# Talking-heads attention with soft mixture of experts, fp32, one core: TensorE's order within a pair of query blocks, pinned, twelve slots for rows, and the norm of mu made per batch

## Chip, cores and metric

The kernel runs on one core of a Trainium2 chip. The metric is the device time of one execution in microseconds. Before the change it is 9190.56 us, the median of three runs (9187.51, 9190.56 and 9199.91).

## The reference

The input x is 4 x 2048 x 256 in fp32, with 16 heads of 16 in the attention and 16 experts of 16 slots each in the mixture. In short, for each of the four batches:

```python
q, k, v = split(x @ Wqkv.T + bqkv)          # 16 heads of 16; rope on q and k
l = einsum('bhij,gh->bgij', q @ k.T * SCALE, Wpre)   # heads mixed before the softmax
a = einsum('bhij,gh->bgij', softmax(l), Wpost)       # and after it
x = layernorm(x + (a @ v) @ Wout.T + bout)
xn = layernorm(x) * gamma + beta
logits = (xn / |xn| * scale) @ (mu / |mu|)  # |mu| over the 256 rows of each of 256 columns
# dispatch = softmax over tokens' experts, combine = softmax over all slots;
# gelu experts on the dispatched slots, combined back
x = layernorm(x + combine(experts(dispatch(xn))))
```

## The kernel before

A batch is done in three stages, one batch after another: `qkv` (projections and rope, about 80 us), `attention` (2058 to 2068 us from the first q k to the last product with v) and `moe` (the mixture and both norms around it, about 160 us). Everything is fp32. Each fp32 matmul appears as two weight loads and two passes in the trace.

The attention walks over 128 **pairs** n of a batch. A pair is two blocks x of 8 query rows, and a block holds 16 heads x 8 queries = 128 rows. The 2048 keys are split into two halves j. TensorE has four kinds of work per pair:

- **q k** (tile `s`, L366, `raw_banks`): the raw scores of a pair. 16 matmuls on 32x32 tiles of the array per half, over all four row groups r and four column groups q, in the order r, then q. Row group r writes PSUM bank r of the four that it takes. The four banks are copied to `raw` in SBUF (L529 on DVE, L532 on ACT).
- `raw_rows` (L388) then moves `raw` into `rows` by eight DMAs of 256 KB on SP's queue, which brings the heads of a query onto the partitions. The DMAs of x=0 and x=1 and of halves j=0 and j=1 go into four separate slots of the ring `rows`.
- **Wpre** (tile `l`, L406, `logits`): 16 matmuls on 32x32 tiles per half mix the heads of those rows; they go through row groups 0 to 3 in turn and write two tiles (x = 0, 1) of two banks each. DVE takes each tile's maximum (`top`, L421) and ACT the exponential with that maximum as bias (`expo`, L430), written over the same slot of `rows`.
- `shares` and `weights` put the maxima and sums of both halves together (DVE L441 and L455, ACT L444, POOL L443 to L458) into `w`, which holds Wpost with the softmax's factors in it.
- **mixing** (tile `t`, L478, `mix`): 16 matmuls of 128x128 per half mix the heads behind the softmax and transpose; the four banks go to `aT` by DVE and ACT.
- **v's product** (tile `o`, L498, `values`): 64 matmuls, 128x32 tiles, for half of the heads of one group of 32 query rows in each pair; two copies (L509, L510) put it into `aoT`. After every eighth pair, `finish` (L522 on) multiplies 128 rows by Wout (`pz`), adds the residual `xr` and takes the norm's statistics.

PSUM has four banks with tag `t`, shared in turn by q k, mixing, v's product and `pz`, and two tiles of two banks for Wpre. A matmul that gets a bank waits until what was in it has been copied out.

The order within an iteration n is written out: for each half j, Wpre of pair n, q k of pair n+2, then mixing of pair n-1, block x = j, both of its halves; after the second half `raw_rows(n + 2)` and v's product; at the end the shares. The engines' copies, maxima and exponentials are pinned to that order by `keep_in_program_order` (`keep`); the matmuls, the reciprocal, the two copies of v's product and the shares are not, though the trace shows the phases in the order given. The ring `rows` has ten slots of which a pair takes four; `raw`, `w` and `aT` have two. A second ring `k1` of six slots serves qb (the queries, made by POOL at L343 two pairs ahead), `aoT`, and short-lived tiles of the other two stages. The normalised mu (`mun`) is made once at the start (L134 to L145) and stays in SBUF.

In `moe`, DVE takes the statistics of the norm over 16 tiles (L229, L235), ACT the root (L237), and the normalised rows go through POOL (L604, L605) and ACT (L607) before TensorE has its next work. The stores of the output (L711) and the loads of the next batch's x (L251) share SP's queue.

Of the kernel before, what the change touches and what calls it, by code (L numbers as in the profile page):

```python
# [25 lines left out]
def kernel(  # L26
# [35 lines left out]
    ROWS = 10  # L62
# [38 lines left out]
    mu_sb = work.tile([P, KC, ES], F32, tag="rows", name="mu_sb", bufs=ROWS)  # L101
    nc.scalar.dma_start(mu_sb, mu.rearrange("(c p) e -> p c e", p=P))
# [5 lines left out]
    ones = work.tile([P, P], F32, tag="k1", name="ones", bufs=6)  # L108
    nc.gpsimd.memset(ones, 1.0)
# [23 lines left out]

    sq = work.tile([P, KC, ES], F32, tag="rows", name="sq", bufs=ROWS)  # L134
    nc.vector.tensor_mul(sq, mu_sb, mu_sb)
    pn = ps_t.tile([P, 512], F32, tag="t", name="pn")
    for c in range(KC):
        nc.tensor.matmul(pn[:, :ES], ones, sq[:, c], start=(c == 0), stop=(c == KC - 1))
    rmu = work.tile([P, ES], F32, tag="k1", name="rmu", bufs=6)
    nc.scalar.activation(rmu, pn[:, :ES], AF.Sqrt)  # L140
    nc.vector.tensor_scalar_max(rmu, rmu, NORM_EPS)
    nc.vector.reciprocal(rmu, rmu)
    mun = const.tile([P, KC, ES], F32, tag="mun", name="mun")
    for c in range(KC):
        nc.vector.tensor_mul(mun[:, c], mu_sb[:, c], rmu)  # L145


# [13 lines left out]

    def k1(shape, name):
        return work.tile(shape, F32, tag="k1", name=name, bufs=6)
# [85 lines left out]
    def load_x(b, t, name):  # L249
        xt = work.tile([P, D], F32, tag="x", name=f"{name}_{b}_{t}", bufs=2)  # L250
        nc.sync.dma_start(xt, x[b, ts(t, P), :])  # L251
        return xt


    def qkv(b):
        room = work.tile([P, NT * HEADS * GI], F32, tag="aT", name=f"wq_{b}")
        wqkv_sb, bqkv_sb, rope_sb = carve(room, [KC, 3 * D], [3 * D], [NT, 4 * HH])
        nc.scalar.dma_start(wqkv_sb, wqkvT.rearrange("(c p) n -> p c n", p=P))
        nc.scalar.dma_start(bqkv_sb, bqkv.partition_broadcast(P))
        nc.scalar.dma_start(rope_sb, rope.rearrange("(t p) k -> p t k", p=P))  # L260
        qT = seq.tile([P, NT, KC, P], F32, tag="qT", name=f"qT_{b}")
        kT = seq.tile([P, KC, N], F32, tag="kT", name=f"kT_{b}")
        v = seq.tile([P, NT, D], F32, tag="v", name=f"v_{b}")

        def project(t):
            xt = load_x(b, t, "x")
            px = ps_t.tile([P, 4, P], F32, tag="t", name=f"px_{b}_{t}")
            for c in range(KC):
                nc.tensor.transpose(px[:, c, :], xt[:, ts(c, P)], ident)
            xT = k1([P, KC, P], f"xT_{b}_{t}")  # L270
            nc.scalar.copy(xT, px[:, :KC, :])
            pqk = ps_t.tile([P, 512], F32, tag="t", name=f"pqk_{b}_{t}")
            pv = ps_t.tile([P, 512], F32, tag="t", name=f"pv_{b}_{t}")
            for c in range(KC):
                nc.tensor.matmul(
                    pqk[:, : 2 * D], xT[:, c, :], wqkv_sb[:, c, : 2 * D],
                    start=(c == 0), stop=(c == KC - 1),
                )
            for c in range(KC):
                nc.tensor.matmul(  # L280
                    pv[:, :D], xT[:, c, :], wqkv_sb[:, c, 2 * D :],
                    start=(c == 0), stop=(c == KC - 1),
                )
            qk = k2([P, 2 * HEADS, 2, HH], f"qk_{b}_{t}")
            nc.vector.tensor_add(  # L285
                qk.rearrange("p h a d -> p (h a d)"), pqk[:, : 2 * D], bqkv_sb[:, : 2 * D]
            )
            nc.vector.tensor_add(v[:, t, :], pv[:, :D], bqkv_sb[:, 2 * D :])

            cc = rope_sb[:, t, : 2 * HH].unsqueeze(1).to_broadcast([P, 2 * HEADS, 2 * HH])  # L290
            ss = [
                rope_sb[:, t, (2 + a) * HH : (3 + a) * HH].unsqueeze(1).to_broadcast([P, 2 * HEADS, HH])
                for a in range(2)
            ]
            r = k2([P, 2 * HEADS, 2, HH], f"r_{b}_{t}")
            s = k2([P, 2 * HEADS, 2, HH], f"s_{b}_{t}")
            nc.vector.tensor_mul(
                r.rearrange("p h a d -> p h (a d)"), qk.rearrange("p h a d -> p h (a d)"), cc
            )
            for a in range(2):  # L300
                nc.gpsimd.tensor_mul(s[:, :, a, :], qk[:, :, 1 - a, :], ss[a])  # L301
            nc.vector.tensor_add(r, r, s)
            return r.rearrange("p h a d -> p (h a d)")

        def turn(t, r):
            pr = ps_t.tile([P, 4, P], F32, tag="t", name=f"pr_{b}_{t}")
            for c in range(2 * KC):
                nc.tensor.transpose(pr[:, c, :], r[:, ts(c, P)], ident)
            nc.vector.tensor_copy(qT[:, t], pr[:, :KC, :])
            nc.scalar.copy(kT[:, :, ts(t, P)], pr[:, KC:, :])  # L310

        r = project(0)
        for t in range(NT):
            nxt = project(t + 1) if t + 1 < NT else None
            turn(t, r)
            r = nxt
        return qT, kT, v


    def attention(b, y, qT, kT, v):  # L320
        keep = tc.keep_in_program_order
        st = new_stats(f"a{b}")
# [4 lines left out]
        def pair_q(n):  # L327
# [4 lines left out]
            qb = k1([P, KC, 2, 4, 2, 2, 2], f"qb_{b}_{n}")  # L332
# [18 lines left out]
        def raw_banks(n, c, engs):  # L351
# [11 lines left out]
            for r in range(4):  # L363
                rows = slice(32 * r, 32 * (r + 1))
                for q in range(4):
                    nc.tensor.matmul(  # L366
# [7 lines left out]
            return [lambda r=r: engs[r](raw[:, 4 * c + r, :], prs[r]) for r in range(4)]  # L374
# [15 lines left out]
        def logits(n, j):  # L390
# [11 lines left out]
            for x in range(2):  # L402
                for h in range(2):
                    for q in range(4):
                        c = (q + 2 * x + h) % 4
                        nc.tensor.matmul(  # L406
# [29 lines left out]
        def shares(n):  # L436
# [4 lines left out]
            nc.vector.tensor_tensor(m, m2[:, :, 0:1], m2[:, :, 1:2], ALU.min)  # L441
            f = small.tile([P, 2, 2], F32, tag="f", name=f"f_{b}_{n}")
            nc.gpsimd.tensor_tensor(f, m.to_broadcast([P, 2, 2]), m2, ALU.subtract)  # L443
            nc.scalar.activation(f, f, AF.Exp)  # L444
# [6 lines left out]
        def weights(n):  # L451
# [3 lines left out]
            nc.vector.reciprocal(z, z)  # L455
# [12 lines left out]
        def mix(n, x, j, engs):  # L468
# [5 lines left out]
            e = s["e", j][x]  # L474
            for r in range(2):
                pt = ps_t.tile([P, 4, P], F32, tag="t", name=f"t_{b}_{n}_{x}_{j}_{r}")
                for a in range(4):
                    nc.tensor.matmul(  # L478
                        pt[:, a, :], e[:, ts(4 * r + a, P)], s["w"][:, 2 * x + j, :],
                        start=True, stop=True,  # L480
                    )
                t0 = j * HT + 4 * r
                engs[r](
                    aT[grp][:, t0 : t0 + 4, :, ts(k, IB)],
                    pt.rearrange("p a (g i) -> p a g i", i=IB),
                )

        outT = {}

        def values(grp, hf):  # L490
# [4 lines left out]
            for t in range(NT):  # L495
                for c in range(4):
                    g0 = 2 * (4 * hf + c)
                    nc.tensor.matmul(  # L498
# [7 lines left out]
            if part == 0 and hf == 0:  # L506
                outT[it] = k1([P, KC, P], f"aoT_{b}_{it}")
            dst = outT[it][:, hf, ts(part, GI)]
            nc.vector.tensor_copy(dst, po[:, 0, :])  # L509
            nc.vector.copy_predicated(dst, odd, po[:, 1, :])  # L510
            if hf == 1:
                aT.pop(grp)
                if part == P // GI - 1:
                    finish(it)

        def finish(it):
            oT = outT.pop(it)
            xt = load_x(b, it, "xr")
            nc.gpsimd.tensor_add(xt, xt, bout_sb)
            pz = ps_t.tile([P, 512], F32, tag="t", name=f"pz_{b}_{it}")  # L520
            for c in range(KC):
                nc.tensor.matmul(  # L522
                    pz[:, :D], oT[:, c, :], wout_sb[:, c, :], start=(c == 0), stop=(c == KC - 1)
                )
            nc.vector.tensor_add(y[:, it, :], pz[:, :D], xt)
            norm_stats(y[:, it, :], it, st)
# [8 lines left out]
        nop = [lambda: None] * 4  # L535
        for n in range(2):
            for c in range(KC):
                for f in raw_banks(n, c, (V, S_, V, S_)):
                    f()
            raw_rows(n)  # L540
        for n in range(n_pairs + 3):
            cur, nxt, prv = n < n_pairs, n + 2 < n_pairs, 0 < n <= n_pairs

            grp, hf = divmod(n - per - 1, per)
            val = 0 <= grp < N // GI
            for j in range(2):
                if cur:
                    logits(n, j)
                fs = raw_banks(n + 2, j, (S_, V, S_, V if j == 0 else S_)) if nxt else nop
                if prv and j == 0:  # L550
                    weights(n - 1)
                if cur:
                    top(n, j, 0)
                fs[0]()
                fs[1]()
# [3 lines left out]
                fs[2]()  # L559
                fs[3]()  # L560
                if cur:
                    expo(n, j, 1)
                if prv:
                    mix(n - 1, j, 0, (V, S_))
                    mix(n - 1, j, 1, (V, S_))
                    if j == 1:
                        state.pop(n - 1)
                if j == 1:
                    if nxt:
                        raw_rows(n + 2)  # L570
                    if val:
                        values(grp, hf)
            if cur:
                shares(n)
# [5 lines left out]
    def moe(b, y):  # L580
# [9 lines left out]
        gamma_sb, beta_sb, b2_sb, hd = carve(room, [D], [D], [ES // P, D], [NP, 2 * S])  # L590
# [4 lines left out]
        nc.gpsimd.memset(hd, 0.0)  # L595
        st = new_stats(f"m{b}")
        for t in range(NT):
            norm_stats(y[:, t, :], t, st)
        mv, rstd = norm_finish(st, f"m{b}")
        xn = seq.tile([P, NT, D], F32, tag="v", name=f"xn_{b}")  # L600
        ss = small.tile([P, NT], F32, tag="ss", name=f"ss_{b}", bufs=2)
        for t in range(NT):
# [3 lines left out]
            junk = k1([P, D], f"sq_{b}_{t}")  # L606
# [6 lines left out]
        for t in range(NT):  # L613
            u = k1([P, D], f"u_{b}_{t}")
# [32 lines left out]
        hb = k1([P, NP, 2 * S], f"hb_{b}")  # L647
# [22 lines left out]
        def slot_weights(t):  # L670
# [7 lines left out]
            ce = k1([P, ES], f"ce_{b}_{t}")  # L678
# [6 lines left out]
        def combine(t, ce, rz):  # L685
# [3 lines left out]
            cT = k1([P, ES // P, P], f"cT_{b}_{t}")  # L689
# [83 lines left out]
```

## Time and profile before

One execution was profiled. Its own figures:

| | |
|---|---|
| time of the profiled execution | 9193.65 us |
| its span, first to last instruction | 9191.9 us |
| mean granted TensorE clock | 0.977 |
| granted clock in the attention (200 to 2100 us) | 1.00 |
| matmul rows of mixing, L478 | 3945.4 us busy, 32768 |
| q k, L366 | 1766.5 us busy, 32768 |
| Wpre, L406 | 1413.8 us busy, 32768 |
| v's product, L498 | 1024.6 us busy, 65536 |
| first q k to last v's product, four batches | 2062, 2058, 2068, 2064 us |
| eight moves of rows per pair, L388 | 4096 DMAs of 256 KB, DMA share 0.57 in the attention |

A row of the profile names the line, the engine, the operation, the tile written and the tiles read. "PE" is a matmul pass, "PEld" a weight load, "SPq" SP's DMA queue. An arrow `<-` in the waits names what ended the idle time of an engine; "issue" stands where the profile shows nothing that it waited for. The timeline has the start in us, the length in us and the instruction, several alike in a row put together with their number behind an x.

### The profile page before, as it was taken

The numbers are of one execution on the slowest core, as the hardware profiler recorded it, in microseconds if no ns is written. First come the engines' busy times: TensorE is split into PE (matmuls) and PEld (weight loads), VectorE is DVE, ScalarE is ACT, GpSimd is POOL, SyncE is SP. The second block draws the span as 40 slices with busy tenths as digits, with TensorE's granted clock in tenths as the row PEclk, the third lists the DMA queues.
The fourth block names the chain that finished last, engine by engine and source line by source line (L and its number), as shares of the span: only waits on it lengthen the run. The fifth ranks groups of instructions, "written<-read, shape, count | busy, mean of one in ns | idle before, by whom it ended". The sixth has DMA issues, their size and how long they took to land. (4 is left out here: it accounts for less than half of the span.)

```text
span 9191.9 us, 373485 instructions
## 1 busy us (share of the span) xinstructions
PE 8249.7 (90%) x166484; PEld 6122.8 (67%) x166484; DVE 5541.1 (60%) x9074; ACT 4961.1 (54%) x9758; POOL 1845.8 (20%) x6481
## 2 busy tenths in 40 slices
PE   7999999997899999999689999999968999999996
PEld 4666776675576677676556676767755666776675
DVE  5666666665666666666466666666645666666664
ACT  3555555553455555555345555555534555555553
POOL 2221222111221122211122211221112221122211
PEclk9999999998999999999899999999989999999998
DMA  4555555552455555555145555555514555555551
GB/s 104 136 136 136 136 133 136 133 139 53 111 136 132 136 136 134 135 135 136 48 112 135 136 137 134 136 134 134 136 45 113 135 135 135 136 138 133 136 135 45
DMA packets 654551, 1140.00 MB, mean 124 GB/s; under 512 B 95760, under 2 KB 127120, under 8 KB 652944
## 3 DMA queue, kind: packets, MB, share of 16 engines
q1 hardware_dynamic: 616704, 1099.18, 49.7%
q8 instruction: 1309, 21.45, 1.0%
q10 hardware_dynamic: 36240, 16.93, 0.7%
q14 instruction: 298, 2.44, 0.1%
HBM read 33.71 MB, written 8.39 MB: 5 GB/s over the span
## 5 line engine op out<-in xcount | busy, mean ns | idle before, releaser
L478 PEld LDWEIGHTS t<-w,rows 128*128 128x128 f32 x32768 | 3760.5, 193 | 1352.9 <-ACT raw L532 753.0
L478 PE MATMUL t<-w,rows 128*128 128x128 f32 x32768 | 3945.4, 279 | 444.0 <-ACT raw L532 439.1
L421 DVE TENSOR_REDUCE m<-l 128x1 f32<-128x1024 f32 x2048 | 2497.0, 1220 | 970.2 <-PE l L406 970.2
L532 ACT COPY raw<-s 128x512 f32<-128x512 f32 x2552 | 1445.6, 590 | 2782.7 <-PE s L366 1646.9
L430 ACT ACTIVATE rows<-l,m 128x1024 f32<-128x1024 f32 x2048 | 2315.1, 1130 | 68.4 <-DVE m L421 60.8
L366 PE MATMUL s<-kT,qb 32*32 32x512 f32 x32768 | 1766.5, 606 | 72.3 <-issue 61.6
L529 DVE COPY aT<-t 128x512 f32<-128x512 f32 x2048 | 1396.6, 682 | 354.5 <-PE t L478 353.7
L532 ACT COPY aT<-t 128x512 f32<-128x512 f32 x2048 | 1219.5, 596 | 596.8 <-PE t L478 596.6
L406 PE MATMUL l<-rows,wmix_sb 32*32 32x512 f32 x32768 | 1413.8, 601 | 59.6 <-issue 35.1
L529 DVE COPY raw<-s 128x512 f32<-128x512 f32 x1544 | 1055.3, 684 | 194.6 <-PE s L366 163.3
L366 PEld LDWEIGHTS s<-kT,qb 32*32 32x32 f32 x32768 | 667.2, 103 | 738.1 <-issue 485.5
L498 PE MATMUL o<-aT,v 128*32 128x64 f32 x65536 | 1024.6, 220 | 17.8 <-issue 17.8
L498 PEld LDWEIGHTS o<-aT,v 128*32 128x32 f32 x65536 | 941.4, 110 | 80.1 <-issue 19.1
L343 POOL TENSOR_TENSOR qb<-qT,hmask 128x16 f32<-128x16 f32 (+3 forms) x3584 | 650.5, 221 | 1437.5 <-PE s L366 1437.5
L443 POOL TENSOR_TENSOR f<-m,m 128x4 f32<-128x4 f32 x512 | 102.8, 201 | 3850.3 <-DVE m L441 3850.3
L455 DVE RECIPROCAL z<-z 128x2 f32<-128x2 f32 x512 | 85.1, 166 | 860.8 <-POOL z L448 860.8
L458 POOL TENSOR_TENSOR w<-wblk_sb,f 128x512 f32<-128x512 f32 x512 | 533.5, 1042 | 40.1
L406 PEld LDWEIGHTS l<-rows,wmix_sb 32*32 32x32 f32 x32768 | 337.8, 103 | 301.6 <-issue 139.9
L509 DVE COPY aoT<-o 128x32 f32<-128x32 f32 x512 | 98.3, 192 | 673.9 <-PE o L498 673.9
L430 ACT ACTIVATION_READ_ACCUMULATOR rows<-l,m 128x1 f32 x2048 | 435.7, 213 | 0.0
L446 POOL TENSOR_TENSOR zf<-f,z 128x4 f32<-128x4 f32 x512 | 103.2, 202 | 762.1 <-ACT f L444 762.1
L301 POOL TENSOR_TENSOR s<-qk,wq 128x256 f32<-128x256 f32 x128 | 115.8, 924 | 497.4 <-DVE qk L285 484.7
(122 smaller groups left out, 2620.4 us busy)
## 6 DMA issues: line engine op xcount, KB each, us to landing
rows<-raw SPq DMA_DIRECT2D x4096, 256.0 KB
x<-in_x_dram SPq DMA_DIRECT2D x64, 128.0 KB
xr<-in_x_dram SPq DMA_DIRECT2D x64, 128.0 KB
out_dram<-qT SPq DMA_DIRECT2D x16, 512.0 KB
wm<-in_w_dram ACTq DMA_DIRECT2D x8, 512.0 KB
wm<-in_w_dram ACTq DMA_DIRECT2D x4, 1024.0 KB
wq<-in_wqkvT_dram ACTq DMA_DIRECT2D x4, 768.0 KB
wq<-in_bqkv_dram ACTq DMA_DIRECT2D x4, 384.0 KB
```

The source lines that it names most:

```text
L301: nc.gpsimd.tensor_mul(s[:, :, a, :], qk[:, :, 1 - a, :], ss[a])
L343: nc.gpsimd.tensor_tensor(qb[:, :, g, s0:s1, :, :, x].rearrange("p c s i h -> p c (s i) h"), qT[:, t, :, i0:i1].unsqueeze(3).to_broadcast( ...
L366: nc.tensor.matmul(prs[r][32 * q : 32 * (q + 1), :], qb[rows, c, q % 2].rearrange("p s i h x -> p (s i h x)"), kT[rows, c, ts(q, QN)], sta ...
L406: nc.tensor.matmul(pls[x][32 * c : 32 * (c + 1), ts(h, 512)], wmix_sb[32 * q : 32 * (q + 1), :], raws[n][j][x][32 * q : 32 * (q + 1), ts(h ...
L421: nc.vector.tensor_reduce(s["m2"][:, x, j : j + 1], s["l", j][x], AX.X, ALU.max, negate=True)
L430: nc.scalar.activation(s["e", j][x], s["l", j][x], AF.Exp, bias=s["m2"][:, x, j : j + 1], accum_out=s["z2"][:, x, j : j + 1],)
L446: nc.gpsimd.tensor_tensor(zf, f, z2, ALU.mult)
L458: nc.gpsimd.tensor_tensor(w, wblk_sb.rearrange("p g i -> p (g i)").unsqueeze(1).to_broadcast([P, 4, HEADS * IB]), f.rearrange("p x j -> p ...
L478: nc.tensor.matmul(pt[:, a, :], e[:, ts(4 * r + a, P)], s["w"][:, 2 * x + j, :], start=True, stop=True,)
L498: nc.tensor.matmul(po[32 * c : 32 * (c + 1)].rearrange("p a i -> p (a i)"), v[:, t, g0 * HD : (g0 + 2) * HD], at[:, t, g0 : g0 + 2, :].rea ...
L529: keep(nc.vector.tensor_copy(dst, src))
L532: keep(nc.scalar.copy(dst, src))
```

## The change

The order of an iteration becomes: v's product, then for each half j q k of pair n+2, Wpre of pair n, (where due, `pz` with its add and statistics), and mixing of pair n-1, now half j of both blocks. All attention matmuls, the reciprocal, both copies of v's product and the shares are pinned with the rest. Raw's four banks go to ACT, DVE, ACT, DVE in both halves, and mixing's four to ACT, DVE, ACT, DVE, the last one always to DVE; DVE copies both of its raw banks ahead of the maxima. The product with Wout is put off by one iteration, and its residual rows are loaded ahead, with the first half of the last v's product before it. The product with v of a group comes one iteration later than before, so the loop is one longer.

The ring `rows` gets twelve slots. `k1` is given up: qb has its own three buffers, `aoT` one, `xr` one, and the short-lived tiles of the other stages take slots of `rows`. The tile of the normalised mu is no longer kept: each batch loads mu into the room `wn` and norms it between the statistics of the norm and its root.

```diff
-    ROWS = 10
+    ROWS = 12
...
-    mu_sb = work.tile([P, KC, ES], F32, tag="rows", name="mu_sb", bufs=ROWS)
-    nc.scalar.dma_start(mu_sb, mu.rearrange("(c p) e -> p c e", p=P))
...
-    sq = work.tile([P, KC, ES], F32, tag="rows", name="sq", bufs=ROWS)
-    nc.vector.tensor_mul(sq, mu_sb, mu_sb)
...
+        def matmul(*args, **kw):
+            keep(nc.tensor.matmul(*args, **kw))
...
-            qb = k1([P, KC, 2, 4, 2, 2, 2], f"qb_{b}_{n}")
+            qb = work.tile([P, KC, 2, 4, 2, 2, 2], F32, tag="qb", name=f"qb_{b}_{n}", bufs=3)
...
+            if part == P // GI - 1 and hf == 0:
+                xt = work.tile([P, D], F32, tag="x", name=f"xr_{b}_{it}", bufs=1)
+                xs[it] = load_x(b, it, xt)
+                nc.gpsimd.tensor_add(xt, xt, bout_sb)
             if hf == 1:
                 aT.pop(grp)
                 if part == P // GI - 1:
-                    finish(it)
+                    todo.append(it)
...
-        for n in range(n_pairs + 3):
+        for n in range(n_pairs + 4):
             cur, nxt, prv = n < n_pairs, n + 2 < n_pairs, 0 < n <= n_pairs
-            grp, hf = divmod(n - per - 1, per)
-            val = 0 <= grp < N // GI
+            grp, hf = divmod(n - per - 2, per)
+            if 0 <= grp < N // GI:
+                values(grp, hf)
             for j in range(2):
+                raw = raw_banks(n + 2, j) if nxt else nop
                 if cur:
                     logits(n, j)
-                fs = raw_banks(n + 2, j, (S_, V, S_, V if j == 0 else S_)) if nxt else nop
                 if prv and j == 0:
                     weights(n - 1)
+                while todo:
+                    finish(todo.pop())
+                t0 = mix(n - 1, 0, j) if prv else nop
+                t1 = mix(n - 1, 1, j) if prv else nop
+                for f, eng in zip(raw, (S_, V, S_, V)):
+                    f(eng)
                 if cur:
                     top(n, j, 0)
-                fs[0]()
-                fs[1]()
+                t0[0](S_)
                 if cur:
                     expo(n, j, 0)
                     top(n, j, 1)
-                fs[2]()
-                fs[3]()
+                t0[1](V)
+                if j == 0:
+                    t1[0](S_)
                 if cur:
                     expo(n, j, 1)
-                if prv:
-                    mix(n - 1, j, 0, (V, S_))
-                    mix(n - 1, j, 1, (V, S_))
                     if j == 1:
-                        state.pop(n - 1)
+                        shares(n)
+                if j == 1:
+                    t1[0](S_)
+                t1[1](V)
                 if j == 1:
                     if nxt:
                         raw_rows(n + 2)
-                    if val:
-                        values(grp, hf)
-            if cur:
-                shares(n)
+                    if prv:
+                        state.pop(n - 1)
...
+        nc.gpsimd.memset(ones, 1.0)
+        nc.scalar.dma_start(mun, mu.rearrange("(c p) e -> p c e", p=P))
         st = new_stats(f"m{b}")
         for t in range(NT):
             norm_stats(y[:, t, :], t, st)
+        nc.gpsimd.tensor_mul(sq, mun, mun)
+        pn = ps_t.tile([P, 512], F32, tag="t", name=f"pn_{b}")
+        for c in range(KC):
+            nc.tensor.matmul(pn[:, :ES], ones, sq[:, c], start=(c == 0), stop=(c == KC - 1))
+        nc.scalar.activation(rmu, pn[:, :ES], AF.Sqrt)
+        nc.vector.tensor_scalar_max(rmu, rmu, NORM_EPS)
+        nc.vector.reciprocal(rmu, rmu)
+        for c in range(KC):
+            nc.vector.tensor_mul(mun[:, c], mun[:, c], rmu)
```

## Prediction

> **What bounds the kernel now.** I read the page first (busy shares, the chain that ended last), then the waits, then one pair of the attention in the timeline, pass by pass on TensorE.
>
> ```profile
> PE 8249.7 (90%) x166484; PEld 6122.8 (67%) x166484; DVE 5541.1 (60%) x9074; ACT 4961.1 (54%) x9758; POOL 1845.8 (20%) x6481
> ...
> PE t L478 11%; PE l L406 3%; PE s L366 2%; DMA rows<-raw 2%; PE o L498 2%; ACT raw L532 1%; SPq L388 0%; PE pz L522 0%; PE pf L693 0%; PE l_d L183 0%; PE o_d L222 0%; POOL xn L604 0%; POOL xn L605 0%; DVE qT L696 0%; DVE st_f L229 0%
> ```
>
> TensorE is the bound, with DVE and ACT at 60% and 54%; the chain runs through TensorE's four phases. What TensorE waits for, from the waits of the whole span (us in total, times, longest):
>
> ```profile
> PEld t L478 <- ACT raw L532: 753.0, 558, 1.6
> ...
> PEld t L478 <- issue: 585.4, 456, 2.1
> PEld s L366 <- issue: 485.5, 1157, 2.3
> ...
> PE t L478 <- ACT raw L532: 439.1, 900, 1.2
> ```
>
> Mixing waits for ACT to empty q k's first bank in nearly every half. The second kind, "issue", is taken up below. One regular pair, TensorE's rows of the timeline (start, length, instruction):
>
> ```profile
> 1001.11 1.22 PE L406 MATMUL l<-rows,wmix_sb 32*32 32x512 f32 x32
> 1001.99 1.49 PE L366 MATMUL s<-kT,qb 32*32 32x512 f32 x32
> 1003.93 3.84 PE L478 MATMUL t<-w,rows 128*128 128x128 f32 x32 [0.45 <-ACT raw L532]
> 1007.70 1.99 PE L498 MATMUL o<-aT,v 128*32 128x64 f32 x128
> 1009.62 1.22 PE L406 MATMUL l<-rows,wmix_sb 32*32 32x512 f32 x32
> 1010.51 1.54 PE L366 MATMUL s<-kT,qb 32*32 32x512 f32 x32
> 1012.58 3.81 PE L478 MATMUL t<-w,rows 128*128 128x128 f32 x32 [0.54 <-ACT raw L532]
> 1016.32 1.22 PE L406 MATMUL l<-rows,wmix_sb 32*32 32x512 f32 x32
> 1017.20 1.49 PE L366 MATMUL s<-kT,qb 32*32 32x512 f32 x32
> ```
>
> From start to start a pair is: mixing 3.74 and 3.77, v's product 1.92, Wpre 0.89 and 0.88, q k 2.07 and (1017.20 to the next mixing at 1019.14) 1.94: 15.21 us. The change leaves mixing and v's product as they are (9.43), so what it can move is the block of Wpre and q k: **2.96** behind v's product (first half), **2.82** behind mixing (second half). Four batches of 128 pairs make 512 pairs: 0.1 us a pair is 51 us, 0.56% of the span. First q k to last v's product takes 2058 to 2068 us a batch, 8252 of 9191.9.
>
> **The new order, walked through.** Now mixing's first bank waits for q k's first bank to be copied (1003.29, 0.59 long, mixing at 1003.93). With Wpre between them, that copy lies beside Wpre: this wait goes. What is late next is the other side: q k's fourth bank. Four banks go round, so q k's rows 0 to 2 find banks that were emptied long ago, but row group 3 takes the bank of whatever came just before: mixing's last bank (second half) or v's product's (first half). Before, Wpre stood in that place and covered those copies. Their rows:
>
> ```profile
> 1009.76 0.19 DVE L509 COPY aoT<-o 128x32 f32<-128x32 f32 x1 [1.27 <-PE o L498]
> 1009.99 0.19 DVE L510 COPY_PREDICATED aoT<-odd,o 128x32 f32<-128x32 int32 x1
> ...
> 1016.43 0.59 ACT L532 COPY aT<-t 128x512 f32<-128x512 f32 x1 [0.82 <-PE t L478]
> ```
>
> Second half: mixing's last result is there 0.11 after the next phase could start (1016.32 to 1016.43); the copy is now DVE's, 0.68 (its own row, mean 682 ns), and 0.05 to TensorE: row group 3 starts at 0.84, or 0.87 with the lag seen in the walk. First half: v's product is copied in two steps ending at 1010.18, 0.56 after 1009.62; row group 3 starts at 0.61. Behind the waiting matmul stand its three neighbours, then all of Wpre, then mixing. Every fp32 matmul here passes its tile twice, 0.43 us each time (Wpre's first tile at 1001.561 in its second pass, q k on the same tile at 1001.991). So Wpre's fourth matmul, the first on row group 3, starts 0.05 + 0.86 behind the wait: 1.78 and 1.52.
>
> What the other twelve do is the unknown. The one row that shows a held matmul in this queue: q k's first stands at 1001.991, its second only at 1002.184, 0.19 later, the rest 17 ns apart. If 0.19 is the cost of any hold, the twelve start at 1.97 and 1.71, their second pass ends about 1.0 later, and mixing follows at 3.04 and 2.78 (second half +0.22, first half -0.18 against 2.82 and 2.96). But Wpre's last second pass began at 1001.741 and so ended at 1002.17: the 0.19 may as well be that wait, which is absent in the new order. Then mixing follows at 2.79 and 2.53 (-0.03 and -0.43). I take the middle: +0.09 and -0.31.
>
> The Trainium skill, in "TensorE: Matmul & The Clock Gate", under "What overlaps and what doesn't", says that weights load beside running matmuls only if the row group differs. The trace has q k's third weights loading 17 ns after the second's, in the same row group, while that runs, so the rule is too strict here; taken literally it would free the twelve early and give the second reading. "TensorEngine Tiling (Array Packing)", under "PSUM Bottleneck", speaks against the change: packing speeds matmuls and leaves the copies as they are. By it alone a half trades an exposed 0.59 copy for an exposed 0.68, some 0.09 x 512 = 46 us worse.
>
> **Stalled pairs.** Only 207 of 500 pair periods are 15.21; the mean is about 15.9. Every eighth pair is 17.43 (the output product pz), 0.28 a pair; 0.46 a pair is irregular, about 1 us in each of half the pairs. Such a one:
>
> ```profile
> 1233.71 1.42 PE L366 MATMUL s<-kT,qb 32*32 32x512 f32 x25
> ...
> 1236.15 1.06 PE L366 MATMUL s<-kT,qb 32*32 32x512 f32 x7 [1.02 <-issue]
> ...
> 1237.14 0.64 PEld L478 LDWEIGHTS t<-w,rows 128*128 128x128 f32 x3 [0.84 <-issue]
> ```
>
> "Issue" has no releaser, but an instruction fetch (queue q8 of the page, 16 KB a piece) starts at 1233.74 and lands just before 1236.15. It comes behind the 384 instructions of v's product, Wpre and q k, which run in some 3.5 us. The new order has the same 384 in one run. Where the fetch ends the block, a shorter block is worth nothing: from the refill to mixing it is 0.99 now and about 1.05 then. So I give the first half's gain to half of the pairs: -0.15. With the second half's +0.09: **-0.06 a pair, -31 us**; the ends are +0.13 (+67) and -0.24 (-123).
>
> **The other parts.**
> - Twelve row slots: the rows of half 1 no longer wait for mixing two phases later (the profile has SPq waiting 4526 us for it). All eight moves (0.55 to 0.6 us each on SP) are then out by about 1.7 us into the next iteration, over 10 us before Wpre reads them; before, four of them landed 7 to 12 us later still. What this can save is real waits on rows or on raw: about 0.05 a pair (7 DVE waits of 1 us in 119 pairs). -26 us, ends 0 and -50.
> - pz, now ahead of mixing instead of behind v's product: 2.22 each before. Its DVE add (0.42) and statistics (0.43) now stand ahead of raw's copies, up to 0.2 late: +6 us, ends -30 and +30.
> - mu's norm per batch: four matmuls, POOL's memset and product, ACT's root and mu's transfer lie beside the statistics of the norm (2166 to 2171 us); DVE's own part follows there: 0.30 + 1.75 + 2 x 0.42 = 2.9 us (rows of the start-up), DVE being the chain in this stage: +12 us for four. If the transfer were late, up to 3 us more each. At the start the same steps go: -3, ends 0 and -5.
> - x's loads: of the next batch only the first now precedes the four output stores on SP, whose issue waits for the last norm (2312 to 2316 us); the second tile's px was at 2309.13. DVE is at that norm until about 2316 anyway (v's add at 2315.79), so of some 9 us at most 6 show: +10 for three, ends 0 and +20.
> - Slots shared with the row ring, fixed qb, pinned vector work: DVE's order keeps mixing's last copy free of a queue (max ends 2.4, copy due 3.9 after mixing's start) and w is ready on POOL about 0.3 to 0.5 before mixing needs it: nothing.
>
> **Sum.** -31 - 26 + 6 + 12 - 3 + 10 = -32: 9193.65 (profiled execution; its span of 9191.9 and 1.75 around it) becomes 9161.7. That execution is 3.1 above the median of 9190.56, so the forecast is **9159 us**, 0.35% faster. Under 0.2%, about 18 us, a measurement can't tell it from no change.
>
> **Rivals.**
> - The held queue costs nothing extra (second reading), 9193.65 - 123 - 1 - 3.1 = **9066**. For: the end of Wpre's pass explains the 0.19 to within 0.02. With Wpre's later matmuls even passing the held one, blocks of 2.69 and 2.43 in every pair give -0.66 x 512 = -338, 8850. Against: stalls are then a larger part of what is left.
> - Slower: the hold at row group 3 costs 0.19 each time and is the longer path in both halves, +67 - 1 - 3.1: **9256**. It decides from the point where row group 3 starts over 0.65 after mixing's end; DVE's 0.68 copy alone makes that. For: the copy used to lie beside 0.88 of Wpre.
> - Slower by fetches: if a fetch falls into every pair's block and not into half of them, the other 256 pairs lose the first half's gain (0.31) and about 1 us less the 0.4 for which row group 3 waits there anyway: 0.91 x 256 = +233, **9392**. It decides where the run of 384 instructions is left with no pause before its end. For: the 456 and 1157 waits for "issue" show how near the queue is to empty. Against: the number of instructions stays the same.
> - The change doesn't do what it says: the traced order of before is already its written one, so that pinning moves nothing, and if the two waits weigh the same, the new order does nothing either: 9190.
>
> **Chances.** Forecast 0.35 (0.25 faster, 0.10 within 0.2%), free queue 0.22, hold 0.25, fetches 0.13, nothing 0.05 (0.03 within, 0.02 slower). Faster 0.47, same 0.13, slower 0.40. Range 8930 to 9350: it leaves out the passing end of the free queue and half of the fetch case. Signs are mixed; the likeliest case alone spans 9110 to 9200.
>
> **What would show it.** Right: the wait of mixing for raw's copy is gone; q k, with 24 of its 32 passes at once, stops before its last row group for the aT copy or aoT; block starts 2.65 and 2.9 apart; 17.4 stays the period with pz. Wrong: blocks under 2.5 (free queue), over 3.0 in both halves (hold), or "issue" well over 585 + 485 us in t and s together (fetches). DMA waits of l on rows would refute the slots' part.

## The result, and the profile after

The changed kernel takes **9642.91 us** (median of four, 9631.98 to 9649.74) against 9190.4 of the kernel before: ratio **1.0489** (95% interval 1.0471 to 1.0508). The forecast was 9159, with 9350 as its upper end: wrong in sign, and outside the range. The profiled execution has a span of 9647.9 us against 9191.9, 456 longer. Its stages say where:

| | before | after | change |
|---|---|---|---|
| start, or issue of the last store, to the first q k (four batches) | 94.8, 68.8, 69.1, 69.0 | 138.5, 116.1, 116.1, 116.0 | +185 |
| first q k to last product with v | 2062, 2058, 2068, 2064 | 2127, 2137, 2131, 2126 | +269 |
| all the rest (mixture, stores) | | | +2 |

From the page, the shares and the lines of the chain:

```profile
PE 8814.4 (91%) x166496; PEld 6396.2 (66%) x166496; DVE 5921.2 (61%) x9589; ACT 4752.3 (49%) x9256; POOL 1856.4 (19%) x6488
...
PE t L302 10%; PE l L302 4%; PE s L302 4%; PE o L302 2%; DMA rows<-raw 0%; ACT rows L412 0%; DVE raw L514 0%; DVE m L403 0%; PE pf L697 0%; PE l_d L162 0%; PE o_d L201 0%; PE pz L302 0%; POOL xn L608 0%; SPq L370 0%; POOL xn L609 0%
```

All attention matmuls now stand on the helper's line, L302, so they are told apart by their tiles. TensorE is still the chain, and "busy" for longer with nearly the same instructions (166496 passes): a busy share does not show that passes stand still. The waits of the whole span:

```profile
PEld t L302 <- ACT raw L517: 419.2, 500, 0.8
PEld s L302 <- issue: 417.3, 537, 3.6
PEld s L302 <- DVE aT L514: 310.9, 500, 0.7
...
PEld l L302 <- issue: 269.9, 275, 2.8
```

The wait of mixing's passes for raw's copy (439 us before) is gone, and q k's wait for mixing's last copy has come, 500 times and 0.7 us at most, as walked. The 419 us of mixing's weight loads are no wait for that copy: in the pair below ACT's copies are through by 1012.34, and mixing starts at 1013.08, behind Wpre. But "issue" now reaches 3.6 us. A regular pair in the timeline:

```profile
1003.60 1.33 PE L302 MATMUL s<-kT,qb 32*32 32x512 f32 x28
...
1006.38 3.84 PE L302 MATMUL t<-w,rows 128*128 128x128 f32 x32
1010.14 1.49 PE L302 MATMUL s<-kT,qb 32*32 32x512 f32 x28
...
1013.08 3.84 PE L302 MATMUL t<-w,rows 128*128 128x128 f32 x32
1016.84 1.99 PE L302 MATMUL o<-aT,v 128*32 128x64 f32 x128
```

The first block is 2.78 and the second 2.94 long. Over all four batches the medians are **2.77 and 2.93**, where they were 2.96 and 2.82, and the regular pair is 15.16 in place of 15.21. So the walk of the regular pair held. Summed from start to start over the four batches, the second blocks take 135 us more, the first blocks and pz together 83, and mixing 57. Of the 135, the regular 0.11 a pair explains 56; the rest lies in the pairs with pz (below). The first blocks should have gained 0.19 a pair, some 97 us; stalls took that and more. A stalled pair:

```profile
884.64 1.11 PE L302 MATMUL s<-kT,qb 32*32 32x512 f32 x24
...
885.00 0.19 DVE L493 COPY_PREDICATED aoT<-odd,o 128x32 f32<-128x32 int32 x1
...
888.37 0.18 PEld L302 LDWEIGHTS s<-kT,qb 32*32 32x32 f32 x5 [3.53 <-issue]
...
888.40 1.07 PE L302 MATMUL s<-kT,qb 32*32 32x512 f32 x4 [2.65 <-issue]
...
892.21 1.57 PEld L302 LDWEIGHTS t<-w,rows 128*128 128x128 f32 x7 [1.67 <-issue]
```

q k stops after 24 passes, where row group 3 waits for the bank of v's product. That bank is copied out by 885.19, so it isn't what holds q k. An instruction fetch starts at 885.44 and its packet takes 1.28 us; q k resumes at 888.37; mixing starts 7.57 us after the block's begin. Counting a first block as stalled where two weight loads of q k or Wpre start over 0.75 us apart, there are 218 (160 before), with a mean block of 4.74 (4.10 before); in all of them a fetch on q8 starts ahead of the next instruction, by 2.69 us in the mean (2.60 before). Four windows of the same trace (length, engines' busy time, granted clock, DMA share, GB/s): v's product and the first block of the regular pair above, then the stop and what follows it:

```profile
1001.70:1003.60 1.90, 1.90 (x129) 1.81 (x128) 0.69 (x1) 0.76 (x4) 0.40 (x2) 1.00 1.06 252
1003.60:1006.40 2.80, 2.80 (x72) 1.25 (x65) 1.81 (x6) 1.07 (x2) 1.24 (x2) 1.00 1.04 237
884.00:888.00 4.00, 1.75 (x76) 0.75 (x64) 1.15 (x4) 1.07 (x2) 1.24 (x2) 0.96 1.05 246
888.00:892.00 4.00, 3.60 (x40) 1.10 (x40) 0.69 (x1) 0.00 (x0) 0.00 (x0) 0.50 0.18 44
```

The DMA engines are full during v's product and the whole first block: the eight moves of rows now go in one burst just there. The same two stretches of the regular pair before, v's product and the first block:

```profile
1007.70:1009.60 1.90, 1.90 (x129) 1.83 (x128) 0.75 (x2) 0.59 (x1) 1.24 (x3) 1.00 0.72 154
1009.60:1012.60 3.00, 2.46 (x73) 1.01 (x65) 2.17 (x5) 0.75 (x2) 0.00 (x0) 1.00 0.84 218
```

So the engines were busy there before too, if less, with four moves and not eight in a row. And behind the stop the granted clock is 0.50: a long stall costs a second time.

What the moves waited for, SP's queue between 200 and 2000 us of the changed kernel:

```profile
SPq L370 <- DVE raw L514: 983.1, 110, 14.4
...
SPq L370 <- PE t L302: 32.6, 46, 1.6
```

Before, in the same window, it waited 1019.5 us for mixing, 451 times. That wait had spread the moves: with ten slots half of a pair's moves could go only when mixing had freed slots. Around 1007 the kernel before issues four (1006.05 to 1009.03) and the next four from 1014.64 to 1017.66; the changed kernel issues the eight of a pair from 1012.88 to 1019.08.

The other 185 us are in the projection stage. Timeline of the changed kernel there:

```profile
2475.39 0.37 ACT L288 COPY kT<-pr 128x256 f32<-128x256 f32 x1 [5.90 <-DVE qT L287]
2475.65 0.38 ACT L249 COPY xT<-px 128x256 f32<-128x256 f32 x1
2476.08 0.30 PEld L253 LDWEIGHTS pqk<-wq,xT 128*128 128x128 f32 x2 [3.28 <-ACT xT L249]
```

and of the kernel before:

```profile
2340.39 0.37 ACT L271 COPY xT<-px 128x256 f32<-128x256 f32 x1 [1.45 <-PE px L269]
2342.59 0.37 ACT L310 COPY kT<-pr 128x256 f32<-128x256 f32 x1 [1.83 <-DVE qT L309]
2344.41 0.37 ACT L271 COPY xT<-px 128x256 f32<-128x256 f32 x1 [1.45 <-PE px L269]
```

After the change ACT copies the next tile's transpose only behind kT of an earlier one, and the projection's weights wait 3.28 us for it; a tile takes 6.5 us there (2475.39 to 2481.93) against 4.0 before (2340.39 to 2344.41). In the row ring a tile of x takes five slots (x, xT, qk, r, s), twelve slots are less than three tiles, and x's load waits for r of an earlier tile.

### The profile page after: what moved, and what is told of

Same layout as the page of the kernel before. It is cut to its first block, busy times and chain, and to the rows that moved or that the text cites. A ratio compares the mean times of both kernels' runs of the same rounds, so it can differ in the third digit from the quotient of the medians.

```text
span 9647.9 us, 372315 instructions
## 1 busy us (share of the span) xinstructions
PE 8814.4 (91%) x166496; PEld 6396.2 (66%) x166496; DVE 5921.2 (61%) x9589; ACT 4752.3 (49%) x9256; POOL 1856.4 (19%) x6488
## 3 DMA queue, kind: packets, MB, share of 16 engines
q8 instruction: 1308, 21.43, 1.0%
## 5 line engine op out<-in xcount | busy, mean ns | idle before, releaser
L302 PEld LDWEIGHTS t<-w,rows 128*128 128x128 f32 x32768 | 3796.1, 194 | 877.6 <-ACT raw L517 419.2
L302 PE MATMUL t<-w,rows 128*128 128x128 f32 x32768 | 3983.9, 280 | 43.6 <-issue 23.9
L403 DVE TENSOR_REDUCE m<-l 128x1 f32<-128x1024 f32 x2048 | 2415.1, 1219 | 344.6 <-PE l L302 341.8
L302 PE MATMUL l<-rows,wmix_sb 32*32 32x512 f32 x32768 | 2224.3, 609 | 144.6 <-issue 127.0
L302 PE MATMUL s<-kT,qb 32*32 32x512 f32 x32768 | 2021.0, 609 | 156.5 <-issue 121.0
L514 DVE COPY raw<-s 128x512 f32<-128x512 f32 x2048 | 1368.1, 689 | 762.5 <-PE s L302 673.5
L517 ACT COPY raw<-s 128x512 f32<-128x512 f32 x2048 | 1107.6, 589 | 1389.8 <-issue 1146.6
L302 PEld LDWEIGHTS l<-rows,wmix_sb 32*32 32x32 f32 x32768 | 897.1, 104 | 585.2 <-issue 269.9
L302 PE MATMUL o<-aT,v 128*32 128x64 f32 x65536 | 1021.9, 220 | 19.8 <-issue 19.7
L302 PEld LDWEIGHTS s<-kT,qb 32*32 32x32 f32 x32768 | 406.5, 104 | 952.1 <-issue 417.3
L302 PEld LDWEIGHTS o<-aT,v 128*32 128x32 f32 x65536 | 938.9, 110 | 81.5 <-issue 20.8
L253 PE MATMUL pqk<-wq,xT 128*128 128x512 f32 x256 | 180.6, 844 | 173.7 <-ACT xT L249 157.7
L438 POOL TENSOR_TENSOR f<-f,z 128x4 f32<-128x4 f32 x512 | 103.3, 202 | 888.9 <-DVE z L437 888.9
```

Of the source, the lines that this page charges most:

```text
L253: nc.tensor.matmul(pqk[:, : 2 * D], xT[:, c, :], wqkv_sb[:, c, : 2 * D], start=(c == 0), stop=(c == KC - 1),)
L302: keep(nc.tensor.matmul(*args, **kw))
L403: nc.vector.tensor_reduce(s["m2"][:, x, j : j + 1], s["l", j][x], AX.X, ALU.max, negate=True)
L438: nc.gpsimd.tensor_tensor(f, f, z.to_broadcast([P, 2, 2]), ALU.mult)
L514: keep(nc.vector.tensor_copy(dst, src))
L517: keep(nc.scalar.copy(dst, src))
```

## The experiments

All were timed beside the kernel before, whose medians there lay between 9173 and 9186 us. Ratios are to that, with the 95% interval.

**Own buffers for x.**

```diff
-            xt = load_x(b, t, k2([P, D], f"x_{b}_{t}"))
+            xt = load_x(b, t, work.tile([P, D], F32, tag="x", name=..., bufs=2))   # xr: bufs=2 too
-            xT = k2([P, KC, P], f"xT_{b}_{t}")
+            xT = work.tile([P, KC, P], F32, tag="w", name=..., bufs=2)
```

> The changed kernel, but x and its transpose in the projection stage no longer take slots of the row ring: x has two buffers of its own (shared with xr), the transpose the two of w. Ring theory: the projection stage, 113 to 119 us between the first and last transposes' starts against 66 before, goes back to about 66, so four times 45 us come back: about 9460 from 9643. Rival (x's loads stand behind the output stores on SP): at most 20 us back, about 9620. The attention stays at 2126 to 2137 us a batch in both.

9471.2 us, 1.0311 (1.0295 to 1.0326): 172 us back. From the issue of the last store to the first q k it is 65.5 us, against 68.8 in the kernel before; over the four batches these stages give back 199 us, and the attention takes 17 more (2133 to 2138 a batch). The ring it was.

**Ten slots.** As above, with `ROWS = 10`.

> As e1_own_x with ten row slots in place of twelve: half of a pair's moves of rows wait for mixing again. Theory that the eight moves in one burst slow the instruction fetch (157 packets run beside one fetch against 116 before): the stalled first blocks shrink by 0.3 us or more, 65 us or more under e1_own_x. Fetch position theory (only where the fetch falls matters): within 30 us of e1_own_x. If ten slots cost waits on rows, over 30 us slower.

9141.51 us, 0.9952 (0.9935 to 0.9968): 330 us less than with twelve, and 0.5% under the kernel before. Stalled first blocks: 165, mean 3.95 (227 and 4.76 with twelve). Far more than the 65 us named: it is the moves, or the slots. The DMA engines are still nearly full in a first block (0.92 over its first 2.7 us in the mean, 1.04 with twelve slots), so a full stretch alone isn't what costs.

**Moves held.** Twelve slots, `raw_rows` taken from the end of an iteration into the next one:

```diff
                 if cur:
                     top(n, j, 0)
+                if j == 0 and 0 < n < n_pairs - 1:
+                    held = raws[n + 1]["from"][:, 0, 0:1]
+                    keep(nc.vector.tensor_copy(held, held))
+                    raw_rows(n + 1)
                 t0[0](S_)
```

> As e1_own_x, twelve slots, but the eight moves of a pair are held back: they are issued in the next iteration, after DVE's first maximum, and a copy of one column of raw onto itself on DVE (0.2 us) makes them wait for it. So the slots stay and only the time of the moves goes to where ten slots put them, into mixing. Burst theory (moves issued with v's product and the first block delay the instruction fetch there): within 40 us of e3_ten_slots, 9100 to 9190. Slot theory (twelve slots cost by themselves): within 60 us of e1_own_x, 9410 to 9530.

9137.3 us, 0.9955 (0.994 to 0.997). With twelve slots the time is that of ten, so it is when the moves run that counts, not the slots. The first block of a regular pair and v's product ahead of it, for comparison with the windows above:

```profile
1012.00:1013.90 1.90, 1.90 (x129) 1.83 (x128) 0.69 (x1) 0.81 (x4) 0.40 (x2) 1.00 0.42 99
1013.90:1016.70 2.80, 2.80 (x71) 1.15 (x64) 1.76 (x6) 1.07 (x2) 1.24 (x2) 1.00 0.00 0
```

DMA 0.42 and 0.00 in place of 1.06 and 1.04. Stalls that remain: 137, mean 3.79. In them a fetch takes as long as in the burst (1.24 us with 6 packets of moves starting beside it, 1.19 with 157 under twelve slots in one burst), so the moves don't slow a fetch that runs. But it starts 1.23 us ahead of the stop, against 0.57, and the gap between weight loads is 1.40 in place of 2.12: the later start is nearly the whole difference. The granted clock from 200 to 2000 us is 1.00 again (0.99), and mixing behind a first block lasts 3.77 in the mean (3.92).

**Half of the moves held** (those of block x=1; x=0 as in the changed kernel).

> As e5_moves_held, but only the four moves of block 1 are held back; the four of block 0 go as soon as raw is there. Burst theory by amount: about half of the 334 us between e1_own_x and e5_moves_held, 9250 to 9350. Burst theory by length (four moves are through before the first block begins): 9130 to 9190. Slot theory: 9410 or more.

9161.73 us, 0.9989 (0.998 to 0.9999): the second of the burst readings. Four moves are through before the first block (DMA share 0.87 in v's product and 0.04 in the block's first 2.7 us, in the mean), and nearly all of the loss is gone. Here and with ten slots four moves go in a row, and neither loses over 24 us against the held eight; what loses is eight in a row ahead of and beside the first block.

**Moves held and nothing else**, x in the row ring as in the change.

> The changed kernel with nothing but its moves held back (as in e5_moves_held); the projection stage keeps x and its transpose in the row ring. If the two causes are separate and add up: 9643 - 334 = about 9310. If the ring's longer projection stage was partly hidden or shared with the moves, off by more than 40 us.

9328.63 us, 1.0149 (1.0132 to 1.0166): 314 us back against 334 with x's own buffers. The two causes add up to within 20 us: 314 + 172 of 452, with the order and all the rest left 34 or more on the good side.

**v's product inside mixing** (between the two blocks of mixing's first half, its copies behind `t0[1]`; on the first variant).

> As e1_own_x, and v's product moved between the two blocks of mixing's first half, so that 64 passes of mixing stand on both sides of its 256 instructions and q k and Wpre (128) no longer follow it in one run. Fetch theory: the 218 first blocks that stall for instructions (4.74 us in place of 2.77, 429 us in all) mostly vanish; every first block now waits for mixing's last bank as the second does (2.93, +82 us): about 9460 - 350 + 82 = 9190. Rival (the stalls come from the banks and the engines that empty them, or from row moves on the DMA queues): the 429 us stay, 9540 or more.

9417.2 us, 1.0252 (1.0237 to 1.0267): only 54 us back. The first block's stalls do vanish, but v's product is then 2.22 in the mean (1.92), mixing in two parts is 0.2 longer, and both blocks wait for mixing's last bank at 2.93 to 3.01. The stall has partly moved with the fetch: 111 of 504 v's products are over 0.5 longer than the median, where 3 of 496 were on the first variant. Whether it would go in this order with the moves held was not run.

**Old order within the new frame.** Wpre ahead of q k, on the first variant and on the one with ten slots:

```diff
+                if cur:
+                    logits(n, j)
                 raw = raw_banks(n + 2, j) if nxt else nop
-                if cur:
-                    logits(n, j)
```

> As e1_own_x (twelve slots) with Wpre ahead of q k again, all else as changed. Burst theory: the moves slow the fetch in this order too, so it is 200 us or more slower than p4_old_order_ten. Interaction theory (the burst hurts only where q k comes first): within 60 us of p4_old_order_ten.

9975.07 us, 1.0862 (1.0846 to 1.0878).

> As e3_ten_slots with Wpre ahead of q k again: what the order of the two alone is worth, with the copies and pz as in the changed kernel. By the walked blocks (2.96 and 2.82 against 2.77 and 2.93) about 0.08 a pair, 41 us, slower than e3_ten_slots: 9180. If the copies put ahead of the maxima delay mixing in this order, more.

9640.22 us, 1.05 (1.0485 to 1.0516). Twelve slots cost **335 us in the old order too**: no interaction with the new one. That both are slow is another matter: the second block is 3.56, most likely since raw's copies stand ahead of the maxima that are ready first here (in the last run below, where they take turns, it is 2.82).

**The kernel before, pinned,** and **pinned with q k first.** The second adds this:

```diff
+                fs = raw_banks(n + 2, j, ...) if nxt else nop
                 if cur:
                     logits(n, j)
-                fs = raw_banks(n + 2, j, ...) if nxt else nop
...
+                for f in fs:
+                    f()
                 if cur:
                     top(n, j, 0)
```

> The kernel before with the matmuls, the reciprocal, the copies of v's product, the shares and the output product pinned to their written order, and nothing else. Both theories: no change, 9170 to 9210, as the traced order is the written one; only pz, which is slipped between v's product, Wpre and q k in the trace of before, gets one place: 64 times up to 1 us slower.

9312.9 us, 1.0142 (1.0125 to 1.0159): neither theory had that. Pinned where they are written, the shares stand behind v's product, and DVE's minimum waits for its copies. In a regular pair the block starts at 1023.39, the copies at 1023.53 and 1023.75 and the minimum right behind them at 1023.86; w is ready at 1026.68, mixing starts at 1026.73 behind it, and the first block is 3.34 in place of 2.96. The change avoids it, having moved the shares up.

> The kernel before, pinned, with q k issued ahead of Wpre in each half and raw's copies ahead of the maxima; ten slots, its own rings, v's product and pz in their old places, mu once. Fetch theory (the order removes the wait that hid the fetches): the attention is some 200 to 300 us longer, 9400 to 9490. Rival (the order is harmless, the slots, the deferred pz or the new buffers cost the time): 9150 to 9230.

9308.29 us, 1.0134 (1.0119 to 1.015): 5 us from the pinned kernel, with the same late w and 160 stalls (149 there). So the order by itself hardly adds stalls; what it is worth can't be read here, since w hides it.

**pz's add later,** on the variant with held moves.

```diff
                 for f, eng in zip(raw, (S_, V, S_, V)):
                     f(eng)
+                add()        # finish() now issues pz alone and returns these two
                 if cur:
                     top(n, j, 0)
...
                 t0[1](V)
+                stats()
```

> As e5_moves_held, and in the pairs with pz its add on DVE comes behind raw's two copies and its statistics behind the second maximum, in place of ahead of all of them. Theory: in these 64 pairs q k of the second half stands 1.3 us longer (4.23 to 4.29 in place of 2.93) as the maxima, the exponential and ACT's copy of a mixing bank all come late behind the add; then 50 to 85 us come back: 9050 to 9090. Rival (pz's own matmuls and bank are the cost): within 20 us of e5_moves_held.

**9035.08 us, 0.9851 (0.9834 to 0.9867)**, the best of all: 102 us back, more than expected. A pair with pz is 16.36 in place of 17.87 in the mean, and the second blocks are no longer than the others on its account.

**Old order in the best variant,** copies and maxima in turn as before. More differs than the order: mixing's banks go to DVE and ACT in turn again, behind the exponentials, and the held moves go behind raw's last copy.

> As e6_pz_add_later with Wpre ahead of q k again and the copies and maxima taken in turn, as the kernel before has them, so that the order of the two is all that differs. By the walked blocks (2.96 and 2.82 in place of 2.77 and 2.93) 0.08 a pair, about 40 us slower than e6_pz_add_later: 9060 to 9100. If the order is worth nothing, 9020 to 9050; if the new order feeds the fetch stalls, below 9020.

9381.64 us, 1.0211 (1.0196 to 1.0226), 347 us slower than the new order, not 40. The second block is 2.82 as walked; the first has a median of 3.38, with 232 stalls, mean 4.37. It isn't w, which is ready 1.36 us before mixing in the median: mixing's passes wait for ACT's copy of raw, as in the kernel before (89.8 us between 200 and 2000 us). The moves run later here (DMA share 0.74 during v's product in the mean, 0.43 with the new order) and the fetch starts 0.69 us ahead of the stop in place of 1.25, so that the moves may be at work again. What the order alone is worth isn't measured by this run, nor by any other. **That stays open.**

## Why the prediction was wrong, point by point

- **Regular pair: right.** Forecast ranges 2.53 to 2.78 and 2.79 to 3.04 for the two blocks, measured 2.77 and 2.93. The first sits at the "hold" end; the middle values taken were 0.12 and 0.02 too low, 0.14 a pair.
- **Twelve slots: the step that failed.** "All eight moves are then out by about 1.7 us into the next iteration ... -26 us, ends 0 and -50." The time of issue was about right (the last of the eight starts 2.05 us into the iteration in the median), the sign wrong: **+334 us** (own x buffers with twelve slots against the same with held moves), +314 in the changed kernel. I asked when the rows arrive and not what they would run beside. The wait that I counted as a cost had split the moves into two groups of four; without it eight go in a row, through v's product and the first block, where TensorE uses up its instructions fastest (384 in some 3.5 us).
- **Shared slots: the second failed step.** "Slots shared with the row ring ... nothing." It was **+172 us**. I counted the ring for the attention only; the stage that borrows it holds five tiles per step.
- **Fetches.** The stall was named and sized (2.4 us from a fetch to the next instruction, about half of the pairs), and a rival of 9392 stood on it. But its cause was given as the place of the fetch in the run of instructions, and "the number of instructions stays the same" as the reason against. That number did stay the same (1308 fetches, 1309 before); what changed was the traffic around them. While a fetch runs, 157 packets of moves start, against 116 before, and the fetch starts 0.56 us ahead of the stop against 0.98 (1.23 with held moves). The fetch itself takes as long in all three (1.20, 1.14 and 1.24). That a fetch waits in the DMA engines behind moves before it starts fits all of this, but no run shows such a wait itself. One row was misread as well: the fetch at 1233.74 didn't land just before 1236.15, its packet was through at 1234.70, 1.45 us earlier, and that lag is 1.4 to 1.5 us in the mean in all three kernels, with the burst and without. And the sign named for fetches did not come: "issue" in t and s fell from 585 + 485 us to 215 + 417, though the stalls cost more, so these sums don't measure them.
- **Clock.** Not foreseen: behind 25 of the stalls, with 1.9 to 3.2 us between the starts of two passes, the granted clock was 0.50; before the change, and with held moves, behind none. Others as long stayed at full clock. Mixing behind first blocks is 0.15 longer in the mean with the burst than without.
- **pz: +6 forecast.** It went from 2.22 to 3.27 above a regular pair, 2.71 with held moves. Part of the 3.27 is stalls, which fall into these pairs too; with the moves held the term is 0.49 a pair, 31 us in all. It was under its size: the add ahead of raw's copies was named and put at 0.2 us at most, but with the add out of the way a pair with pz is only 1.20 above a regular one.
- **mu per batch: +12 forecast.** The root of that norm comes 9.0 us after the first statistics, 6.4 before: 2.6 a batch, near the 2.9 walked. From the last v's product to the last store's issue the first three batches are not longer than before by more than 0.3 us, so that it is given back behind; the fourth is 4.7 longer.
- **x's loads: +10 forecast.** With x in buffers of its own the stage is 65.5 us against 68.8, so nothing of it shows.

With both failed steps undone, the kernel with held moves has 9137.3, 22 us from the forecast. That nearness is partly luck: the 26 us from the slots (twelve with held moves against ten are worth 4), the walk and pz (both put too low) and the projection stage (shorter, where 10 us more were forecast) are errors of mixed sign, and 137 stalls in place of 160 were not forecast at all.

## What to carry to other kernels

A wait on a buffer also times a transfer. Before taking it away, look at the stretch into which the transfer will move: how long the DMA engines will be full in one go there, and what else fetches through them, instructions too. When tiles are put into a ring that another stage sized, count the slots per step in every stage that uses it; and when work is pinned, look at what each pinned instruction now stands behind.

## What the runs showed of the hardware

- TensorE's instructions come in pieces of 16 KB over the DMA engines (queue q8, 1308 in an execution), and a phase of short instructions can run dry: 2.5 to 2.7 us in the median from the start of a fetch to the next pass, in 132 to 232 first blocks of 512 pairs, by run. Moves beside a fetch don't lengthen it (1.19 us with 157 packets, 1.24 with 6), but with eight moves in a row it starts later against the stop (0.57 us ahead, 1.23 with the moves held). The Trainium skill, "Runtime: NRT & Kernel Launch" under "Instruction fetch mechanics", says that fetches go in blocks of 256 instructions ahead of need and are mostly hidden; the blocks agree (16 KB), the hiding does not here.
- In the stalled pair shown, TensorE was without a pass for 2.65 us, the granted clock fell to 0.50 before it went on (the window up to 888.00 has 0.96), and the next 4 us ran at it. The Trainium skill, "TensorE: Matmul & The Clock Gate" under "What's actually happening", has two states, full and half, with half after an idle window of about 3.4 us; the two states agree with these rows, but a shorter idle time was enough here: 2.65 us for the passes, with the weight loads idle for 3.53 in all.
